# Loading the front of a two-layer graph kernel as 32-wide squares on two DMA queues

## The chip, the cores and the metric

The kernel runs on one core of a Trainium2 chip, in one launch. The metric is the device time of one execution in microseconds (us); of several executions the median counts.

## The reference

Two graph layers over N = 4096 nodes with C = 512 features. `adj` is a 4096 x 4096 matrix of zeros and ones.

```python
# layer 0: mean of the first 64 neighbours, two linear maps
keep = (adj > 0) & (cumsum(adj > 0, axis=1) <= 64);  cnt = keep.sum(axis=1)
nb_mean = (keep @ x) / max(cnt, 1)
xj = leaky_relu(nb_mean @ W_nb.T + b_nb)
xi = leaky_relu(x @ W_line.T + b_line)
x1 = layernorm(x + xi + where(cnt > 0, xj, 0))
# layer 1: graph attention
Wh = x1 @ W + bW
e  = leaky_relu((Wh @ a1 + b1)[:, None] + (Wh @ a2 + b2)[None, :], 0.2), -9e15 where adj == 0
out = layernorm(x1 + softmax(e, axis=1) @ Wh)
```

## The kernel before

The work is cut into 32 blocks of 128 rows. The order of the instructions on each engine is written out by hand; each engine goes through its own list in order, and waits only on semaphores.

**Stages.** (1) The *front* (L444 to L470) loads the first blocks of x and both weights of layer 0's maps. (2) The *maps*, L637 to L668: for each pair of blocks g, `seven(g, ...)` forms y = x W_nb^T and the line x W_line^T of two blocks with seven half-size products in place of eight (L519). (3) The *aggregation*, L726 to L766: for each block i, `keep @ y` with y split into a high and a low part (`y_hi`, `y_lo`, L758), in four groups of eight blocks; the step s counts the groups. (4) Layer 1 (L909, L1095, L1222).

**Turned operands.** TensorE contracts over partitions, so x and the weights are needed with the features on partitions. There are two ways to turn a 128 x 512 block:

- By squares: four DMAs (`load_turned_x`, L298; one for each group of 32 partitions, 64 KB, rows of 512 bytes) bring the block so that one VectorE 32 x 32 transpose (L334) ends it. The blocks 1 to 31 of x come like this.
- By TensorE: `squares` (VectorE copy, L315), four transposes by an identity matrix (`transpose_to`, L157), and a copy out of PSUM (L158, ScalarE or VectorE). x's block 0 (tile `xb`, one plain DMA of 256 KB) and the eight blocks of the two weights (`raw`, plain DMAs of 256 KB each, `load_w`, L360) come like this.

**Queues.** SP and ACT issue DMAs through hardware queues, POOL through a software queue. In the front SP issues x block 0, half of W_nb, the squares of x block 1, half of W_line, and the bias; ACT the other halves of the weights; POOL the squares of the blocks from 2 on. The hardware DMAs use eight completion semaphores in turn, over both queues together: the ninth waits until the first has landed, and so on.

**Order in the front.** TensorE first runs `spin(15)`, fifteen identity transposes, while nothing has come. Then block 0 and three blocks of W_nb are turned, and the first products run; `pys[0]`, `pys[1]` (x blocks 0 and 1 by W_nb) and `pls[0]`, `pls[1]` (by W_line) are called by `linear` (L383), each four products of 128 x 512. `pys[0]` is cut in two pieces among the transposes.

Behind them VectorE forms sums of the weights (`t1`, `t2`, `t4`, `t3`, L525, L526, L541, L542), `y_lo` (L440), turned x (L334), `line(0)` and `line(1)` (L418) and sums of x (L510 to L512). ScalarE bends the lines (L422) and copies the bias into a PSUM bank (`bank_z`, L635), which the second product of `seven(1)` adds to. Later VectorE folds W with a1 and a2 (`fold_w`, L402), and adds the line's parts (L582).

**From the maps to the aggregation.** There is no room for four of the last blocks' y while the maps run, so these are stored to `y_d` (L438) and loaded again by `room_again` (L633, 1 MB, SP's queue), which `seven(NT, True)` calls after `load_late` (three broadcast rows of 256 KB, POOL's queue). SP next issues the transposing loads of the adjacency codes, `load_kt` (L682, tile `ktb`). In the aggregation ScalarE makes `kt` from `ktb` (`make_kt`, L282), two steps ahead; in step 2 it also rounds the reloaded y to its high part (L735), after which VectorE takes the low part (L736):

```python
            make_kt(s + 2)
            if g == 2:
                bend0(i - 1)
            codes_late()
            if s == 2:
                for n in range(0, 4, 2):
                    hi, lo = (t[:, n : n + 2, :] for t in y_again)
                    nc.scalar.copy(hi, lo.bitcast(F32))
```

Of the kernel before, what the change touches and what calls it, by code (L numbers as in the profile page):

```python
# [9 lines left out]
F32 = mybir.dt.float32  # L10
F32R = mybir.dt.float32r
BF16 = mybir.dt.bfloat16
# [8 lines left out]
P = 128  # L21
SQ = 32
# [10 lines left out]
def two_layer_adj_gnn(  # L33
# [104 lines left out]
    with ExitStack() as l0:  # L138
# [8 lines left out]
        ident = big.tile([P, P], F32, name="ident")  # L147
        make_identity(nc, ident)

        def transpose_to(dst, src_of, n, wide, move):  # L150

            if wide:
                pt = ps_acc.tile([P, n, P], F32, name="acc")
            else:
                pt = ps_s.tile([P, n, P], F32, name="pt")
            for k in range(n):
                nc.tensor.transpose(pt[:, k, :], src_of(k), ident)  # L157
            move(dst, pt)  # L158

        loaded = {}  # L160
        edge_of = {}
        seen_of = {}
# [125 lines left out]
        with ExitStack() as la:  # L288
# [6 lines left out]
            xrs, xbs, xts, pys, pls = {}, {}, {}, {}, {}  # L295
            lines, held = {}, []

            def load_turned_x(i, queue=nc.gpsimd):  # L298

                if i < NB:  # L300
                    xrs[i] = late[i % 3].rearrange("p (j c) -> p j c", c=P)
                    for n in range(NC):
                        queue.dma_start(  # L303
                            xrs[i][ts(n, SQ)],
                            x_blk(i)[:, ts(n, P)].rearrange("(j a) c -> a j c", a=SQ),
                        )

            def load_own_x(i, queue):
                xbs[i] = work.tile([P, C], F32, name="xb", bufs=1) if i == 0 else late[2]
                queue.dma_start(xbs[i], x_blk(i))  # L310

            def squares(src):

                t = work.tile([P, C], F32, name="t", bufs=4)
                nc.vector.tensor_copy(  # L315
                    t.rearrange("p (m n b) -> p m n b", m=NC, b=SQ),
                    src.rearrange("p (n m b) -> p m n b", m=NC, b=SQ),
                )
                return t

            def turn_by_pe(dst, src, t=None, wide=False, move=nc.scalar.copy):
                t = squares(src) if t is None else t
                transpose_to(dst, lambda m: t[:, ts(m, P)], NC, wide, move)

            def xt_tile():
                return work.tile([P, NC, P], F32, name="xt", bufs=3)
# [1 line left out]
            def turn_x(i, t=None):  # L328
                if i < NB:
                    xts[i] = xt_tile() if t is None else t  # L330
                    if i == 0:
                        turn_by_pe(xts[i], xbs[i])
                    else:
                        nc.vector.transpose(  # L334
                            xts[i].rearrange("p m (j a) -> p j m a", a=SQ),
                            xrs.pop(i).rearrange("p j (m b) -> p j m b", b=SQ),
                        )


            def early(name):  # L340
                dt = I32 if name == "a" else BF16
                t = adj_p.tile([P, CH], dt, name=name).bitcast(F32)
                return t.rearrange("p (c q) -> p c q", q=C)

            raw = {}
            for name in ("nb", "line"):
                t = early("a")
                raw[name] = [t[:, c, :] for c in range(NC)]
            raw["w"] = []
            for k in range(2):  # L350
                t = early("left")
# [3 lines left out]
            t = early("edge")  # L355
            early_rows += [t[:, c, :] for c in range(NC // 2)]

            def load_w(name, src, queues):
                for c in range(NC):
                    queues[c % len(queues)].dma_start(raw[name][c], src[ts(c, P), :])  # L360

            def spin(n):

                idle = ps_acc.tile([P, P], F32, name="acc")
                for _ in range(n):
                    nc.tensor.transpose(idle, ident, ident)

            def turn_w(name, parts=range(NC)):

                if name not in w_t:  # L370
                    w_t[name] = wp.tile([P, NC, C], F32, name=f"wt_{name}")
                moved = [squares(raw[name][c]) for c in parts]
                for c, t in zip(parts, moved):
                    turn_by_pe(
                        w_t[name][:, :, ts(c, P)], None, t, name == "nb",
                        nc.vector.tensor_copy if name == "nb" and c == 1 else nc.scalar.copy,
                    )

            def linear(lhs_t, name, bank=None, part=slice(0, C), behind_first=lambda: None):

                pl = ps_acc.tile([P, C], F32, name="acc") if bank is None else bank
                for k in range(NC):
                    nc.tensor.matmul(  # L383
                        pl[:, part], lhs_t[:, k, :], w_t[name][:, k, part],
                        start=(k == 0 and part.start == 0),
                        stop=(k == NC - 1 and part.stop == C),
                        skip_group_check=part.stop - part.start < C,
                    )
                    if k == 0:
                        behind_first()  # L390
                return pl

            def load_rows(queue):
# [47 lines left out]
                    y_lo[i], src, y_hi[i].bitcast(F32), ALU.subtract  # L441
                )

            load_own_x(0, nc.sync)  # L444
            load_w("nb", w_nb, (nc.scalar, nc.sync))
            load_turned_x(1, nc.sync)
            load_w("line", w_line, (nc.scalar, nc.sync))
            nc.sync.dma_start(bias_line, b_line.partition_broadcast(P))
            spin(15)


            turn_x(0)
            turn_w("nb", range(3))

            for i in (2, 3):
                nc.vector.memset(late[i % 3][:, 0:1], 0.0)
                load_turned_x(i)
            pys[0] = linear(
                xts[0], "nb", part=slice(0, 3 * P), behind_first=lambda: turn_w("nb", range(3, 4))
            )  # L460
            turn_w("line", range(0, 2))
            linear(xts[0], "nb", pys[0], slice(3 * P, C))
            turn_w("line", range(2, 4))
            turn_x(1)
            load_turned_x(4)
            nc.vector.memset(raw["w"][0][:, 0:1], 0.0)
            load_w("w", w, (nc.sync,))
            load_rows(nc.sync)
            pys[1] = linear(xts[1], "nb")
            pls[0] = linear(xts.pop(0), "line")  # L470

            wide = [pls[0]]

# [154 lines left out]
            def room_again():  # L628
                for y, name in ((y_hi, "hi"), (y_lo, "lo")):
                    t = last.tile([P, ROOM, C], F32R, name=name)  # L630
                    y_again.append(t[:, 0:4, :])
                    y.update((EDGE + n, t[:, n, :]) for n in range(ROOM))
                nc.sync.dma_start(y_again[1].bitcast(F32), y_d)  # L633

            nc.scalar.copy(bank_z, bias_line)  # L635
            idle = [lambda: None] * 4
# [55 lines left out]
        def bend0(i):  # L692
            if i >= 0:
                nc.scalar.activation(fin[i], fin[i], AF.Prelu, alpha=SLOPE)
# [30 lines left out]
        make_kt(1)  # L725
        for s in range(NB * NS):  # L726
            i, g = divmod(s, NS)
            make_kt(s + 2)
            if g == 2:
                bend0(i - 1)  # L730
            codes_late()
            if s == 2:
                for n in range(0, 4, 2):
                    hi, lo = (t[:, n : n + 2, :] for t in y_again)
                    nc.scalar.copy(hi, lo.bitcast(F32))  # L735
                    nc.vector.tensor_tensor(lo, lo.bitcast(F32), hi.bitcast(F32), ALU.subtract)  # L736
            if g == 0:
                load_kt(i + 2)
                if i < 2:
                    accs[i] = ps_s.tile([P, NC, P], F32, name="pt").rearrange(  # L740
                        "p k c -> p (k c)"
                    )
                else:
                    accs[i] = ps_acc.tile([P, C], F32, name="acc")
            if g == 2:
                if i < NB - 1:
                    owns[i] = place("own")
                    nc.sync.dma_start(owns[i], x_blk(i))
            if g == 3 and i < NB - 1:
                nc.gpsimd.dma_start(owns[i], own_d[i], accum_op=ALU.add)  # L750
            kt = kts.pop(s)
            turns = list(range(KB))
            if s == NS - 1:
                turns = turns[:2] + turns[6:] + turns[2:6]
            for n, k in enumerate(turns):
                j = g * KB + k
                for term in (y_hi, y_lo):
                    nc.tensor.matmul(  # L758
                        accs[i], kt[:, k // 2, k % 2, :], term[j],
                        start=(g == n == 0 and term is y_hi),  # L760
                        stop=(g == NS - 1 and n == KB - 1 and term is y_lo),
                    )
            if g == 0:
                finish(i - 2, 4)
            finish(i - 1, g)
            codes_step(start + int((s + 1) * RATE / NS))  # L766
# [584 lines left out]
```

## Time and profile before

| | |
|---|---|
| median of 3 runs | 1555.14 us (1552.86 to 1555.37) |
| the profiled execution | 1554.29 us, of which the span of its instructions is 1552.5 us |
| TensorE (PE) | busy 1541.1 us, 99% of the span |
| VectorE (DVE), ScalarE (ACT), GpSimd (POOL) | 1266.3, 987.2 and 268.1 us |
| granted TensorE clock | 0.999 |

Times in the views count from the start of the span. The chain of waits follows the work that ended last back to what released each step. A line of the timeline gives the start, the busy time, engine, line, operation, tiles and count; `[0.75 <-DVE t L582]` is idle time ahead of it and what ended it. A matmul in 32-bit floats leaves two records. Busy times of one engine overlap a little; the distance between two starts is what an instruction takes of the engine.

### The profile page before, as it was taken

Reading aid. Unit: us, or ns where it says so; the run is one execution under the profiler, and the core shown is the slowest. Engines: PE = TensorE matmul, PEld = TensorE weight load, DVE = VectorE, ACT = ScalarE, POOL = GpSimd, SP = SyncE. Lnnn points to the kernel's source line nnn. Section 1 sums busy time; section 2 is a strip of 40 time slices with the busy share of each in tenths; the row PEclk is TensorE's granted clock in tenths of the full one; section 3 lists DMA queues with packets and bytes.
Section 4 is the critical chain, followed back from the end, with each engine's and each line's share of the span. In section 5 each row is a group of like instructions: output and inputs, shape, how many; then the busy total and the mean of one; then the engine's idle time right before and its main releaser. Section 6 shows DMA issues by size and latency. Waiting matters only on the chain.

```text
span 1552.5 us, 19129 instructions
## 1 busy us (share of the span) xinstructions
PE 1541.1 (99%) x6567; PEld 1239.6 (80%) x6567; DVE 1266.3 (82%) x2350; ACT 987.2 (64%) x1194; POOL 268.1 (17%) x428
## 2 busy tenths in 40 slices
PE   9999999999999999999999999999999999999998
PEld 5444468888888888878888888888888888888886
DVE  6988759989999899478888788888888888888864
ACT  3766668878888887427684567555675556755520
POOL 4544312222212222110001101111011110111101
PEclk9999999999999999999999999999999999999999
DMA  8965588979888886644122112222122221222201
GB/s 237 227 218 184 190 249 243 257 240 264 243 252 231 270 244 198 154 124 115 41 62 57 46 37 69 62 61 48 36 69 63 60 49 34 69 67 57 53 3 55
DMA packets 175889, 203.27 MB, mean 131 GB/s; under 512 B 102112, under 2 KB 135648, under 8 KB 167472
## 3 DMA queue, kind: packets, MB, share of 16 engines
q1 hardware_dynamic: 147616, 131.38, 29.5%
q0 software_dynamic: 26544, 68.69, 17.2%
q10 hardware_dynamic: 1632, 1.98, 0.4%
q8 instruction: 51, 0.84, 0.2%
q14 instruction: 46, 0.38, 0.1%
HBM read 142.08 MB, written 43.13 MB: 119 GB/s over the span
## 4 chain that ended last, share of the span: by engine, by line
PE 96%; DMA 2%; DVE 1%; SPq 0%; issue 0%; ACT 0%; ACTq 0%; POOLq 0%; DVEq 0%; POOL 0%
PE acc L1095 35%; PE acc L758 28%; PE pt L1095 14%; PE acc L519 12%; PE acc L909 4%; PE pt L758 1%; PE acc L383 1%; DMA ktb<-code_d 1%; DMA w<-x_d 1%; DMA a<-in_L_gnn_W_line_dram 0%; SPq L815 0%; DVE c L841 0%; DVE a L841 0%; PE pt L157 0%; DVE st L118 0%
## 5 line engine op out<-in xcount | busy, mean ns | idle before, releaser
L1095 PE MATMUL acc<-bt,s 128*128 128x256 f32 x1504 | 335.7, 379 | 0.0
L1095 PEld LDWEIGHTS acc<-bt,s 128*128 128x128 f32 x1504 | 285.8, 190 | 38.9
L758 PE MATMUL acc<-y_hi,kt 128*128 128x512 f32 x780 | 303.4, 389 | 0.0
L758 PE MATMUL acc<-y_lo,kt 128*128 128x512 f32 x780 | 303.4, 389 | 0.0
L980 ACT ACTIVATE w<-nat,few 128x1024 f32<-128x1024 uint8 x128 | 137.0, 1137 | 237.7 <-DVE a L1055 237.7
L1095 PE MATMUL acc<-bt,a 128*128 128x256 f32 x1056 | 239.0, 379 | 0.0
L1095 PE MATMUL pt<-bt,a 128*128 128x256 f32 x992 | 224.5, 379 | 0.0
L1095 PEld LDWEIGHTS acc<-bt,a 128*128 128x128 f32 x1056 | 200.6, 190 | 27.3
L1095 PEld LDWEIGHTS pt<-bt,a 128*128 128x128 f32 x992 | 188.5, 190 | 25.6
L282 ACT ACTIVATE kt<-ktb,few 128x1024 fp32r<-128x1024 uint8 x124 | 142.9, 1152 | 97.9 <-PE acc L758 78.5
L1055 DVE STREAM_TRANSPOSE a<-w 128x1024 f32<-128x1024 f32 x128 | 153.1, 1226 | 61.8 <-ACT w L1036 51.0
L127 POOL TENSOR_TENSOR rs<-ve,few 128x1 f32<-128x1 f32 x64 | 45.1, 705 | 811.1 <-DVE ve L125 798.3
L758 PEld LDWEIGHTS acc<-y_lo,kt 128*128 128x128 f32 x780 | 146.4, 188 | 30.4
L758 PEld LDWEIGHTS acc<-y_hi,kt 128*128 128x128 f32 x780 | 146.4, 188 | 30.3
L973 ACT ACTIVATE w<-w,st_n 128x1024 f32<-128x1024 f32 x128 | 149.3, 1233 | 16.1 <-DVE m L990 16.1
L1036 ACT ACTIVATE w<-w,nm 128x1024 f32<-128x1024 f32 x128 | 145.5, 1137 | 11.1 <-DVE nm L1027 11.1
L990 DVE CUSTOM_DVE_ANT_0 w<-e_n,w 128x1024 f32<-128x1024 f32 x128 | 149.5, 1221 | 1.3
L179 ACT ACTIVATE edge<-a,few 128x2048 bf16<-128x2048 int32 x64 | 136.3, 2129 | 0.5 <-DMA a<-in_adj_dram 0.5
L227 ACT CAST code<-left 128x2048 uint8<-128x2048 bf16 x64 | 121.1, 1893 | 0.0
L210 DVE TENSOR_TENSOR left<-edge,left 128x2048 bf16<-128x2048 bf16 x64 | 78.4, 1225 | 2.2
L198 DVE TENSOR_TENSOR_SCAN left<-few,ends,left 128x1024 bf16<-128x1024 f32 x32 | 75.2, 2351 | 1.1
L303 POOL DMA_DIRECT2D c<-in_x_dram x120 | 65.8, 555 | 57.0 <-DVE xt L334 40.7
(236 smaller groups left out, 2059.2 us busy)
## 6 DMA issues: line engine op xcount, KB each, us to landing
a<-in_adj_dram SPq DMA_DIRECT2D x64, 1024.0 KB, 6.0
code_d<-code POOLq DMA_DIRECT2D x64, 256.0 KB, 4.0
nat<-code_d SPq DMA_DIRECT2D x248, 64.0 KB, 2.2
w<-x_d SPq DMA_DIRECT2D x128, 64.0 KB, 2.1
own<-in_x_dram SPq DMA_DIRECT2D x31, 256.0 KB, 3.3
own<-own_d POOLq DMA_DIRECT2D x31, 256.0 KB, 5.2
x_d<-own POOLq DMA_DIRECT2D x31, 256.0 KB, 4.8
c<-in_x_dram POOLq DMA_DIRECT2D x120, 64.0 KB, 5.0
```

Of the source, the lines that this page charges most:

```text
L179: nc.scalar.activation(edge_of[s], loaded.pop(s).rearrange("p (t q) -> p q t", q=2), AF.Sigmoid, bias=steep[:, 0:1], scale=STEEP, accum_ou ...
L210: nc.vector.tensor_tensor(left, e, left, ALU.mult)
L227: nc.scalar.copy(code.bitcast(U8).rearrange("p (t q) -> p q t", q=2), seen_of.pop(s))
L282: nc.scalar.activation(kts[s], bytes_.rearrange("p t (i r) -> p t r i", r=2), AF.Sigmoid, bias=steep[:, 1:2], scale=STEEP,)
L519: nc.tensor.matmul(bank, lhs[:, k, :], rhs[:, k, :], start=start and k == 0, stop=k == 1, skip_group_check=True,)
L758: nc.tensor.matmul(accs[i], kt[:, k // 2, k % 2, :], term[j], start=(g == n == 0 and term is y_hi), stop=(g == NS - 1 and n == KB - 1 and ...
L973: nc.scalar.activation(dst, src, AF.Prelu, bias=bias, scale=scale, alpha=0.2)
L980: nc.scalar.activation(wts[b][:, i, :], nats[b, i // 2].bitcast(U8)[:, i % 2, :], AF.Relu, bias=far, scale=-FAR,)
L990: nc.vector.tensor_tensor_reduce(w_i, e2_n, w_i, 1.0, -3e38, ALU.subtract, ALU.max, m4s[b][:, i : i + 1])
L1036: nc.scalar.activation(w_i, w_i, AF.Exp, bias=nms[b][:, i : i + 1], accum_out=z4s[g][:, r, i : i + 1])
L1055: nc.vector.transpose(a[:, r].rearrange("p s (i a) -> p i s a", a=SQ), wts[2 * g + r][:, :, ts(k, 8 * SQ)].rearrange("p i (s x) -> p i s x ...
L1095: nc.tensor.matmul(banks[g][n], lhs[:, j, :], bt[:, 4 * k + j, rhs, :], start=(k == 0 and j == 0 and n == mate[0]), stop=(k == NP - 1 and ...
```

## The change

Block 0 of x and both weights now come as squares too. `load_squares` is the general form of the four DMAs; its list `queues` gives the first two groups of partitions (0 to 63) to SP and the other two (64 to 127) to ACT. A weight comes in two halves of 256 rows, each four DMAs of 128 KB. The order of issue on both queues is x block 0, W_nb's halves, x block 1, W_line's halves, x block 2, then x block 3, which waits until block 0 is turned. On each queue that is two DMAs of each item. POOL's queue loads x from block 4 on.

Weights are turned by VectorE in quarters (128 rows, `turn_quarter`), and `by_quarters` has one quarter of the product (four of 128 x 128) follow each: for `pys[0]` and for `pls[0]`. Fifty-four instructions go: nine VectorE copies, 36 TensorE transposes and nine copies out of PSUM (eight of them on ScalarE). `spin` has 24 transposes. The bias, W and the rows follow on SP's queue behind the squares.

At the other end, the reload of y goes from SP's queue to POOL's, behind `load_late`, and the rounding of y in step 2 stands ahead of `make_kt(4)`.

```diff
-            def load_turned_x(i, queue=nc.gpsimd):
+            def load_squares(dst, src, queues):
+                for n in range(NC):
+                    queues[n * len(queues) // NC].dma_start(
+                        dst[ts(n, SQ)], src[:, ts(n, P)].rearrange("(j a) c -> a j c", a=SQ)
+                    )
+
+            def turn_squares(dst, src):
+                nc.vector.transpose(
+                    dst.rearrange("p m (j a) -> p j m a", a=SQ),
+                    src.rearrange("p j (m b) -> p j m b", b=SQ),
+                )
+
+            def load_turned_x(i, queues=(nc.gpsimd,)):
...
-            def load_w(name, src, queues):
-                for c in range(NC):
-                    queues[c % len(queues)].dma_start(raw[name][c], src[ts(c, P), :])
+            def load_half(name, src, h):
+                load_squares(raw[name][:, ts(h, 2 * NC)], src[ts(h, 2 * P), :], both)
...
-            def turn_w(name, parts=range(NC)):
...
+            def turn_quarter(name, c):
+                turn_squares(w_t[name][:, :, ts(c, P)], raw[name][:, ts(c, NC)])
+
+            def by_quarters(lhs_t, name):
+                bank = None
+                for c in range(NC):
+                    turn_quarter(name, c)
+                    bank = linear(lhs_t, name, bank, slice(P * c, P * c + P))
+                return bank
...
-            load_own_x(0, nc.sync)
-            load_w("nb", w_nb, (nc.scalar, nc.sync))
-            load_turned_x(1, nc.sync)
-            load_w("line", w_line, (nc.scalar, nc.sync))
-            nc.sync.dma_start(bias_line, b_line.partition_broadcast(P))
-            spin(15)
-
-
-            turn_x(0)
-            turn_w("nb", range(3))
-
-            for i in (2, 3):
-                nc.vector.memset(late[i % 3][:, 0:1], 0.0)
-                load_turned_x(i)
-            pys[0] = linear(
-                xts[0], "nb", part=slice(0, 3 * P), behind_first=lambda: turn_w("nb", range(3, 4))
-            )
-            turn_w("line", range(0, 2))
-            linear(xts[0], "nb", pys[0], slice(3 * P, C))
-            turn_w("line", range(2, 4))
+            both = (nc.sync, nc.scalar)
+            load_turned_x(0, both)
+            for h in range(2):
+                load_half("nb", w_nb, h)
+            load_turned_x(1, both)
+            for h in range(2):
+                load_half("line", w_line, h)
+            load_turned_x(2, both)
+            spin(24)
+
+            turn_x(0)
+            load_turned_x(3, both)
+            nc.sync.dma_start(bias_line, b_line.partition_broadcast(P))
+            pys[0] = by_quarters(xts[0], "nb")
             turn_x(1)
             load_turned_x(4)
+            pys[1] = linear(xts[1], "nb")
             nc.vector.memset(raw["w"][0][:, 0:1], 0.0)
-            load_w("w", w, (nc.sync,))
+            for c in range(NC):
+                nc.sync.dma_start(raw["w"][c], w[ts(c, P), :])
             load_rows(nc.sync)
-            pys[1] = linear(xts[1], "nb")
-            pls[0] = linear(xts.pop(0), "line")
+            pls[0] = by_quarters(xts.pop(0), "line")
...
-                nc.sync.dma_start(y_again[1].bitcast(F32), y_d)
+                nc.gpsimd.dma_start(y_again[1].bitcast(F32), y_d)
...
-            make_kt(s + 2)
-            if g == 2:
-                bend0(i - 1)
-            codes_late()
             if s == 2:
                 for n in range(0, 4, 2):
                     hi, lo = (t[:, n : n + 2, :] for t in y_again)
                     nc.scalar.copy(hi, lo.bitcast(F32))
                     nc.vector.tensor_tensor(lo, lo.bitcast(F32), hi.bitcast(F32), ALU.subtract)
+            make_kt(s + 2)
+            if g == 2:
+                bend0(i - 1)
+            codes_late()
```

More of the change, by code (lines that the diff above doesn't have):

```diff
@@ L148, in two_layer_adj_gnn @@
         make_identity(nc, ident)
[L150 to L158, printed above, removed]
         loaded = {}
@@ L296, in two_layer_adj_gnn @@
             lines, held = {}, []
-            def load_turned_x(i, queue=nc.gpsimd):
+            def load_squares(dst, src, queues):
[9 more added lines that the diff above has]
+            def load_turned_x(i, queues=(nc.gpsimd,)):
                 if i < NB:
                     xrs[i] = late[i % 3].rearrange("p (j c) -> p j c", c=P)
[L302 to L305, printed above, removed]
-                        )
+                    load_squares(xrs[i], x_blk(i), queues)
             def load_own_x(i, queue):
-                xbs[i] = work.tile([P, C], F32, name="xb", bufs=1) if i == 0 else late[2]
+                xbs[i] = late[2]
                 queue.dma_start(xbs[i], x_blk(i))
[L312 to L323, printed above, removed]
             def xt_tile():
@@ L330, in turn_x @@
                     xts[i] = xt_tile() if t is None else t
[L331 to L337, printed above, removed]
+                    turn_squares(xts[i], xrs.pop(i))
             def early(name):
-                dt = I32 if name == "a" else BF16
-                t = adj_p.tile([P, CH], dt, name=name).bitcast(F32)
+                t = adj_p.tile([P, CH], BF16, name=name).bitcast(F32)
                 return t.rearrange("p (c q) -> p c q", q=C)
@@ L346, in two_layer_adj_gnn @@
             for name in ("nb", "line"):
-                t = early("a")
-                raw[name] = [t[:, c, :] for c in range(NC)]
+                t = adj_p.tile([P, CH], I32, name="a").bitcast(F32)
+                raw[name] = t.rearrange("p (j q) -> p j q", q=P)
+                w_t[name] = wp.tile([P, NC, C], F32, name=f"wt_{name}")
             raw["w"] = []
@@ L366, in spin, with linear @@
                     nc.tensor.transpose(idle, ident, ident)
-            def turn_w(name, parts=range(NC)):
[L370 to L379, printed above, removed]
+            def turn_quarter(name, c):
[6 more added lines that the diff above has]
+                return bank
+            def linear(lhs_t, name, bank=None, part=slice(0, C)):
                 pl = ps_acc.tile([P, C], F32, name="acc") if bank is None else bank
@@ L388, in linear @@
                     )
-                    if k == 0:
-                        behind_first()
                 return pl
@@ L442, in y_terms @@
                 )
-            load_own_x(0, nc.sync)
-            load_w("nb", w_nb, (nc.scalar, nc.sync))
-            load_turned_x(1, nc.sync)
-            load_w("line", w_line, (nc.scalar, nc.sync))
-            nc.sync.dma_start(bias_line, b_line.partition_broadcast(P))
-            spin(15)
-            turn_x(0)
-            turn_w("nb", range(3))
-            for i in (2, 3):
-                nc.vector.memset(late[i % 3][:, 0:1], 0.0)
-                load_turned_x(i)
-            pys[0] = linear(
-                xts[0], "nb", part=slice(0, 3 * P), behind_first=lambda: turn_w("nb", range(3, 4))
-            )
-            turn_w("line", range(0, 2))
-            linear(xts[0], "nb", pys[0], slice(3 * P, C))
-            turn_w("line", range(2, 4))
+            both = (nc.sync, nc.scalar)
[9 more added lines that the diff above has]
+            load_turned_x(3, both)
+            nc.sync.dma_start(bias_line, b_line.partition_broadcast(P))
+            pys[0] = by_quarters(xts[0], "nb")
             turn_x(1)
             load_turned_x(4)
+            pys[1] = linear(xts[1], "nb")
             nc.vector.memset(raw["w"][0][:, 0:1], 0.0)
-            load_w("w", w, (nc.sync,))
+            for c in range(NC):
+                nc.sync.dma_start(raw["w"][c], w[ts(c, P), :])
             load_rows(nc.sync)
-            pys[1] = linear(xts[1], "nb")
-            pls[0] = linear(xts.pop(0), "line")
+            pls[0] = by_quarters(xts.pop(0), "line")
             wide = [pls[0]]
```

## The prediction

> **What bounds the kernel now.** First the page, for the engine that sets the end; then busy time by stage.
>
> ```profile
> span 1552.5 us, 19129 instructions
> PE 1541.1 (99%) x6567; PEld 1239.6 (80%) x6567; DVE 1266.3 (82%) x2350; ACT 987.2 (64%) x1194; POOL 268.1 (17%) x428
> ```
>
> ```profile
> 0.00:14.20 14.20, 11.98 (x67) 10.19 (x68) 5.30 (x20) 4.91 (x8) 6.37 (x16) 1.00 0.88 247
> 26.60:206.00 179.40, 179.37 (x418) 79.22 (x419) 151.02 (x247) 116.88 (x150) 81.41 (x150) 1.00 0.66 198
> 206.00:221.00 15.00, 14.24 (x62) 11.15 (x61) 3.91 (x5) 8.58 (x10) 2.14 (x4) 1.00 1.06 298
> ```
>
> Columns: stretch, length, then PE, PEld, DVE, ACT, POOL busy, clock, DMA share, GB/s. PE has no idle time in the maps. So whatever brings the maps forward brings the end forward, unless another engine cannot follow. In the first 14.2 us PE is busy too, but partly with work that is no product: spinning and transposes. The chain of waits shows what the front hangs on:
>
> ```profile
> 1.67 5.90 DMA a<-in_L_gnn_W_line_dram
> 8.46 0.91 PE acc L383 x2
> 11.75 0.87 PE pt L157 x8
> 14.39 10.32 PE acc L383 x24
> 24.73 0.70 DVE t L418
> 26.62 15.48 PE acc L519 x35
> ```
>
> Products are in pieces among transposes until 14.2 us; then `pys[1]`, `pls[0]`, `pls[1]` run unbroken to 24.7. From there line(1), its bend and the bank's copy lead into the maps. The aggregation's start, by the same view:
>
> ```profile
> 206.98 9.18 DMA ktb<-code_d
> 217.32 1.04 ACT hi L735
> 218.38 1.24 DVE lo L736
> ```
>
> **The front on TensorE.** The timeline of PE gives every price:
>
> ```profile
> 1.37 3.46 PE L366 MATMUL acc<-ident 128*128 128x128 f32 x15 [1.37 <-POOL ident masks.py:199]
> 12.46 1.06 PE L383 MATMUL acc<-wt_nb,xt 128*128 128x128 f32 x8
> 13.35 1.04 PE L157 MATMUL pt<-ident,t 128*128 128x128 f32 x8
> 14.22 3.60 PE L383 MATMUL acc<-wt_nb,xt 128*128 128x512 f32 x8
> 17.66 7.03 PE L383 MATMUL acc<-wt_line,xt 128*128 128x512 f32 x16
> ```
>
> A spin transpose costs 3.46/15 = 0.231 us; 24 from 1.37 end at 6.91. A quarter (four 128 x 128 products, eight records) costs 13.35 − 12.46 = 0.89, a whole map 17.66 − 14.22 = 3.44. If data never lack: 6.91 + 4 x 0.89 = 10.47 for `pys[0]`, + 3.44 = 13.91 for `pys[1]`, + 3.56 = 17.47 for `pls[0]`, + 3.44 = 20.91 for `pls[1]`. Before, the same point is 17.66 + 2 x 3.44 = 24.54. The bound of the gain is 3.63 us. Cutting `pls[0]` into quarters costs 0.12 of it, counted here.
>
> **Whether data lack.** Up to W_line's second half 0.26 + 1.05 + 0.26 + 1.05 = 2.62 MB come. x block 4 (0.26 MB, POOL's queue) may run beside them, since block 1 is turned by about 10 us: 2.88 MB. The rows of 512 bytes decide the rate. Two stretches of the DMA view, the first with rows of 2 KB alone, the second mostly with squares (367 − 55 = 312 of 416 packets):
>
> ```profile
> DMA packets 662, 1.22 MB, mean 371 GB/s; under 512 B 64, under 2 KB 64, under 8 KB 662
> DMA packets 416, 0.26 MB, mean 260 GB/s; under 512 B 55, under 2 KB 367, under 8 KB 416
> ```
>
> In the densest half microsecond of squares (7.7 to 8.2 us) it is 234 GB/s. Data start at about 2.2 us (the first issue is at 0.75; the stretch's slices fill from there), and a landing is seen about 0.5 later. I take 260, the nearest row: 2.2 + 2.88/0.26 = 13.3, seen at 13.8. Ends: 371 GB/s gives 10.5, 234 gives 15.0. W_nb is through at 2.2 + 1.31/0.26 + 0.5 = 7.7; its third quarter is turned at 8.4, when PE (second quarter done at 8.69) has only just come to it. x block 1 is seen at 8.7, its turn comes behind the fourth quarter, at 9.7. So `pys[1]` does not wait.
>
> VectorE then decides. Behind W_line's second half it has, by distances of starts: two quarters and x block 2, 3 x 0.63; `t1`, `t2` 2.41; two `y_lo` 1.30; x block 3 0.64; line(0) 0.57; three sums 1.20: 8.0 us. line(1) can start at 13.8 + 8.0 = 21.8; PE would allow 21.1. Before it starts at 24.73: 2.9 us earlier (3.6 at 371 GB/s, 1.7 at 234). VectorE is dense from there, and PE meets it again soon:
>
> ```profile
> 40.54 0.30 PEld L519 LDWEIGHTS acc<-hi,xt 128*128 128x128 f32 x2 [0.75 <-DVE t L582]
> ```
>
> so VectorE's 2.9 and not PE's 3.6 goes into the end. Behind that PE has no stall to 206.
>
> What else moves in the front: ACT issues 16 DMAs at about 0.45 us, but its first copy is `y_hi`, which waits for `pys[0]` anyway; 8 copies out of PSUM, 0.59 each, leave it. The bias now stands behind all squares on SP. By the semaphores it issues at about 15 and, at the 4.3 us to landing that the DMA view shows for it, is there at 19.3; line(0) wants it at about 20. W, a1 and the adjacency issue some 3 us later than before; `fold_w` wants its rows at 25, and edge(0) wants the adjacency at 34 to 35, where it lands by about 31. These cost nothing; with the cover gone (bias at 21) line(0) would give back 1 us.
>
> A rule speaks against this front. The Trainium skill, page "DMA: Bandwidth & Descriptors", section "Bandwidth", calls transfers under 64 KB dominated by their descriptors and gives 138 GB/s at 64 KB; by that, an estimate, 2.88 MB would take 20.9 us, line(1) would start near 31.6, and the kernel would lose 7. The row of 260 GB/s, where 64 KB squares were most of the packets, decides. For the division of the queues, the row is that one queue's squares alone ran at 234 GB/s. The page "SBUF — State Buffer", section "Door 1: The DMA port swizzle", says that partitions 0 to 63 reach only half of the 16 ports and 64 to 127 the other half; by that, SP's and ACT's squares together should exceed 234.
>
> **The reload of y.** In the timeline of PE
>
> ```profile
> 218.46 0.44 PE L758 MATMUL pt<-hi,kt 128*128 128x512 f32 x1
> 219.66 0.50 PE L758 MATMUL pt<-lo,kt 128*128 128x512 f32 x1 [0.76 <-DVE lo L736]
> ```
>
> neighbours elsewhere are 0.227 apart. From 218.46 to 221.36 are seven steps, 1.59, in 2.90 us: 1.31 lost. ACT's rounding stands behind `make_kt(4)`, which waits for `ktb` until 216.26, while y has landed at 205.69 + 6.9 = 212.6. In the new order the rounding waits only for y. But y now issues at about 207.3, behind 0.79 MB of rows on POOL's queue and beside two transposing loads (1.05 MB): 2.9 MB in all, which the stretch moved at 298 GB/s, so 206.9 + 9.7 = 216.6 if y is last, 206.9 + 1.84/0.298 = 213.1 if its queue goes first. Middle: about 215; then the low part is ready at 217.3, the product wants it at 217.78, and nearly all of the 1.31 goes. At 216.6 some 0.7 is saved. I take 0.9. `make_kt(4)` ends at about 218.5, wanted at 221. The transposing loads on SP no longer stand behind 1 MB, which has no price: kt(4) has 2 us to spare.
>
> **Sum.** 2.9 + 0.9 = 3.8 against the profiled execution's 1554.29: 1550.5 (its span less 3.8, and the same 1.8 around it). It lies 0.85 below the median of the runs, so 1551.3 is the forecast. A measurement of this kernel tells some 0.2%, 3.1 us, from no change; that is 1552.0 to 1558.3.
>
> **Rivals.** *Data come as fast as PE takes them* (300 GB/s and more, both halves of the ports in use): 3.6 + 1.3 = 4.9, 1550.2. For it: each queue serves other partitions. Against: W_line's squares meet x block 4. 30%.
>
> *The front lands slowly, and the gain shrinks below 3.1*: 234 GB/s gives 1.7, and y as late as 216.6 gives 0.7: 2.4, 1552.7. The kernel would count as the same. 25%.
>
> *Four semaphores to a queue starve the front* (slower). Each queue may have four squares in flight; the fifth waits for the first to land. SP shows such waits now:
>
> ```profile
> SPq L303 <- DMA a<-in_L_gnn_W_nb_dram: 2.6, 2, 2.1
> ```
>
> So x block 0, W_nb's second half, W_line's first half and x block 2 follow one another, landing by landing. At the 4.3 us that the squares on SP take to land now, block 2 is there at 0.75 + 17.2 = 17.95, and line(1), 6.7 behind it, at 24.7: no gain in the front, 1554.2. At the 6.2 us of W_line's loads on ACT it is 25.6 and 32.3: 7.6 late, less 0.9, so 1561.8. The kernel counts as slower from 5.3 us a landing on (22.0, line(1) 4.0 late). Against it: such landings are long where bytes wait for bytes, and then the rate is full; squares with little beside them land in 2.1 (the page's 128 loads of `w`). Four landings of 3.5 fit the forecast's 14.8. 11%.
>
> The change does what it says: the waits of the new order show no wait of VectorE or PE other than for the squares.
>
> **Chances.** The forecast 34%, the fast rival 30%, the small gain 25%, the starved front 11%. The forecast's own lower edge (1551.3 + 0.7) touches 1552.0, so I leave 2 of its points to no change: faster 0.62, same 0.27, slower 0.11. The range takes the fast rival's 1550.2 less 0.5 for a median's luck, and the small gain up to no front gain at all (1555.14 − 0.7 = 1554.4): 1549.7 to 1554.5.
>
> **What would show it.** In the new profile: `pls[1]` ends near 21; line(1) starts at 21 to 22 and waits for PE or follows VectorE's sums without a gap; the last W_line squares land near 13.8; no idle PE between 6.9 and 20.9; near 215 the reload, and PE without the 0.76. Wrong would be: VectorE waiting for W_line beyond 17 us, PE waiting longer at L582 than before, or ACT's rounding waiting for y beyond 217.

## The result: slower, and the profile after

The changed kernel takes 1569.42 us (median of 7 runs, 1560.91 to 1574.83), the kernel before beside it 1554.2; the ratio is 1.009 (95% interval 1.0062 to 1.0118). The forecast was 1551.3, faster. The profiled execution, 1560.91 us, is the fastest of the seven, so it shows only a part of the loss.

In this execution the front did what the prediction says. From the timelines of PE and VectorE, changed kernel:

```profile
14.70 7.17 PE L360 MATMUL acc<-wt_line,xt 128*128 128x128 f32 x40
```

```profile
14.09 1.31 DVE L295 STREAM_TRANSPOSE wt_line<-a 128x512 f32<-128x512 f32 x2 [0.97 <-DMA a<-in_L_gnn_W_line_dram]
21.96 0.68 DVE L393 TENSOR_TENSOR t<-acc,bias_line 128x512 f32<-128x512 f32 x1
26.52 0.69 DVE L377 SCALAR_TENSOR_TENSOR edge<-left,code 128x512 f32<-128x512 f32 x1 [0.98 <-DMA code<-in_L_gnn_a_dram]
28.02 0.69 DVE L377 SCALAR_TENSOR_TENSOR edge<-left,code 128x512 f32<-128x512 f32 x1 [0.81 <-DMA code<-in_L_gnn_a_dram]
```

W_line's second half is turned from 14.09 (forecast 13.8), `pls[1]` ends at 21.7, and line(1), the second line, starts at 21.96, 2.77 earlier than before. That is the earliest of the twelve profiled executions with the new front (this one and those of the runs below): the others turn that half from 14.18 to 15.23 and start line(1) from 22.57 to 23.93 (the four with the old front: 24.04 to 25.27). Then 1.79 is given back: `fold_w` waits for a1 and a2, which now come behind W and the squares. PE meets VectorE again at L552 (L582 before), as busy stretch and wait show:

```profile
39.64 1.98 PE L489 MATMUL acc<-hi,xt 128*128 128x512 f32 x4 [0.80 <-DVE t L552]
```

That product started at 40.54 before. The 0.90 stays, as PE's timeline shows for the aggregation's first product, before and after:

```profile
205.62 0.50 PE L758 MATMUL pt<-y_hi,edge 128*128 128x512 f32 x1
```

```profile
204.72 0.50 PE L728 MATMUL pt<-y_hi,edge 128*128 128x512 f32 x1
```

One pair of executions does not show a gain of that size: the four profiled old fronts (this one, e3, e4 and e10 below) scatter from 204.93 to 206.15 at this point.

Then the reload, first as the DMA view of before has it (KB, us from issue to landing), then in the changed kernel: busy time by stretch (columns as before: length, PE, PEld, DVE, ACT, POOL, clock, DMA share, GB/s), the chain of waits, and PE's timeline:

```profile
lo<-y_d SPq DMA_DIRECT2D x1, 1024.0 KB, 6.9
```

```profile
206.00:221.00 15.00, 11.72 (x52) 9.37 (x50) 0.65 (x2) 2.95 (x3) 0.87 (x2) 1.00 1.11 136
221.00:240.00 19.00, 14.99 (x58) 11.99 (x59) 15.06 (x21) 15.93 (x15) 1.49 (x3) 0.82 1.16 267
224.50:228.50 4.00, 3.49 (x8) 2.46 (x9) 3.94 (x4) 4.00 (x4) 0.89 (x1) 0.52 1.07 313
```

```profile
206.34 17.09 DMA lo<-y_d
225.81 17.56 PE pt L728 x71
```

```profile
217.34 0.39 PE L728 MATMUL pt<-lo,kt 128*128 128x512 f32 x1
224.55 0.79 PE L728 MATMUL pt<-hi,kt 128*128 128x512 f32 x1 [6.82 <-ACT hi L701]
225.81 0.79 PE L728 MATMUL pt<-lo,kt 128*128 128x512 f32 x1 [0.47 <-DVE lo L702]
226.82 0.63 PE L728 MATMUL pt<-lo,kt 128*128 128x512 f32 x1
227.25 0.63 PE L728 MATMUL pt<-hi,kt 128*128 128x512 f32 x1
```

The reload takes 17.09 us; 6.9 before. In its stretch the DMA moves 136 GB/s where it moved 298, with its engines no less busy (1.11 against 1.06). PE waits 6.82 + 0.47, and then its products are 0.43 apart instead of 0.227, until 228.5; the granted clock from 224.5 to 228.5 is 0.52. The 128 products end at 225.81 + 17.56 = 243.37, 38.65 after the first. Unbroken they take 29.31 (the rounding alone, e4 below): 9.34 lost, of which 7.29 are the waits and 2.05 the halved clock. Before, 30.66, so 1.35 lost. Sum: −0.90 + 9.34 − 1.35 = +7.1; the spans differ by 6.6, so half a microsecond comes back later.

The Trainium skill, page "TensorE: Matmul & The Clock Gate", section "Part 1: The HAM clock gate", says that the clock falls to half after an idle window of about 3.4 us and comes back after as long a busy one. The 6.82 idle and the steps of 0.43 agree. The length of the idle time does not bear it out as a threshold: in e12 and e13 below the granted clock falls to 0.5 for 3.4 us after idle times of 2.05 and 1.91. The measurement decides.

### The profile page after: what moved, and what is told of

It reads as the page before. It is cut to its first block, busy times and chain, and to the rows that moved or that the text cites. A ratio compares the mean times of both kernels' runs of the same rounds, so it can differ in the third digit from the quotient of the medians.

```text
span 1559.1 us, 19160 instructions
## 1 busy us (share of the span) xinstructions
PE 1540.4 (99%) x6580; PEld 1240.9 (80%) x6580; DVE 1267.3 (81%) x2347; ACT 982.6 (63%) x1186; POOL 264.6 (17%) x421
## 4 chain that ended last, share of the span: by engine, by line
PE 93%; DMA 3%; DVE 1%; issue 1%; ACT 0%; POOL 0%; ACTq 0%; SPq 0%; POOLq 0%; DVEq 0%
PE acc L1065 35%; PE acc L728 28%; PE pt L1065 14%; PE acc L489 10%; PE acc L879 5%; PE pt L728 1%; DMA lo<-y_d 1%; DMA c<-in_x_dram 1%; DMA code<-in_L_gnn_a_dram 1%; DMA nat<-code_d 0%; DMA a<-in_L_gnn_W_nb_dram 0%; DMA a<-in_L_gnn_W_line_dram 0%; ACT code L217 0%; DMA e_d<-w 0%; POOL own_d L404 0%
## 5 line engine op out<-in xcount | busy, mean ns | idle before, releaser
L1065 PE MATMUL pt<-bt,a 128*128 128x256 f32 x992 | 224.5, 379 | 0.0
L188 DVE TENSOR_TENSOR_SCAN left<-few,left 128x1024 bf16<-128x1024 f32 x32 | 73.3, 2292 | 1.1
```

Of the source, the lines that this page charges most:

```text
L188: nc.vector.tensor_tensor_scan(left[:, 1], three.to_broadcast([P, CH // 2]), left[:, 0], NEIGHBORS + 3.0 if h == 0 else end, ALU.max, ALU. ...
L1065: nc.tensor.matmul(banks[g][n], lhs[:, j, :], bt[:, 4 * k + j, rhs, :], start=(k == 0 and j == 0 and n == mate[0]), stop=(k == NP - 1 and ...
```

## The experiments

"Spread" is lowest to highest. The medians of before in the four groups were 1553.9, 1554.3, 1554.2 and 1553.5.

| run | front | reload on | rounding | store of `wa` | median us (spread) | ratio, 95% interval |
|---|---|---|---|---|---|---|
| e4 | old | SP | new order | 35 us | 1552.8 (1552.0–1555.7) | 0.9995 [0.9986, 1.0003] |
| e10 | old | SP | new order | late | 1553.3 (1552.2–1555.8) | 0.9996 [0.9987, 1.0005] |
| e3 | old | POOL | new order | 35 us | 1565.1 (1562.0–1567.7) | 1.0076 [1.0063, 1.0089] |
| e2 | new | SP | old order | 35 us | 1558.1 (1552.7–1563.0) | 1.0023 [1.0008, 1.0037] |
| e1 | new | SP | new order | 35 us | 1553.1 (1551.5–1561.3) | 1.0002 [0.9990, 1.0014] |
| e7 | new, rows first | SP | new order | 35 us | 1558.7 (1553.2–1563.1) | 1.0025 [1.0013, 1.0038] |
| e5 | new | ACT | new order | 35 us | 1557.4 (1552.0–1563.9) | 1.0020 [1.0004, 1.0035] |
| e8 | new | SP | new order | late | 1551.1 (1549.8–1552.4) | 0.9977 [0.9968, 0.9986] |
| e9 | new, rows first | SP | new order | late | 1552.2 (1551.3–1554.6) | 0.9984 [0.9975, 0.9993] |
| e11 | new | POOL | new order | late | 1563.6 (1561.5–1567.3) | 1.0064 [1.0050, 1.0078] |
| e12 | new | POOL, transposes held | new order | late | 1556.3 (1554.3–1557.5) | 1.0013 [1.0004, 1.0021] |
| e15 | new | POOL, ahead of rows | new order | late | 1552.9 (1551.1–1554.7) | 0.9995 [0.9985, 1.0004] |
| e13 | new | ACT | new order | late | 1551.6 (1550.4–1554.8) | 0.9983 [0.9974, 0.9992] |
| e14 | new | ACT, further behind | new order | late | 1551.7 (1550.8–1553.9) | 0.9989 [0.9979, 0.9998] |

**The change taken apart.** e1 is the changed kernel with the reload back on SP; e2 has the new front alone; e3 the old front with the reload and the rounding changed; e4 the rounding alone.

```diff
-                nc.gpsimd.dma_start(y_again[1].bitcast(F32), y_d)
+                nc.sync.dma_start(y_again[1].bitcast(F32), y_d)
```

> The changed kernel with the reload of y back on SP's queue; front and order of the rounding stay as changed. Theory A (the reload on POOL's queue, beside the transposing loads, is what costs; the front gains 0.9 us): PE's 6.8 us wait for the rounding (ACT hi) is gone, the reload lands about 7 us after its issue, the rounding starts near 212, the 1.31 us of stall that the kernel before has there goes too; 1552 us, about 2 below before. Theory B (the rounding ahead of make_kt(4) is what costs, since ScalarE then waits for y with kt behind it): PE still waits several us there, 1558 or more. Theory C (the front upsets the load traffic all the way to the maps' end): the reload stays slow, over 12 us, 1558 or more.

> The front of the change alone: the reload on SP and the rounding behind make_kt(4), as before. A: maps end 0.9 us sooner than before (204.7 in place of 205.6), the stall of 1.31 us at the reloaded blocks stays; 1553.4, 0.9 below before. B: the same. C: slower than before by some us.

> The kernel before with the other two edits alone: reload on POOL's queue, rounding ahead of make_kt(4). A: the reload lands 15 us or more after its issue, PE waits 7 us and more for ACT hi, time 1562 to 1575 and spread as the changed kernel is. B: the same. C: no such wait, about 1553.

> The kernel before with the rounding ahead of make_kt(4) alone; the reload stays on SP. A: the rounding starts at 212.6, when y has landed, the low part is ready before PE wants it, 1.31 us of stall go: 1553, 1.0 to 1.3 below before. B: PE loses several us, 1558 or more.

The reload's queue carries the loss: e3 has it with the old front, and PE waits 6.4 there for ACT's rounding. The rounding ahead of `make_kt(4)` is harmless, as e4's chain shows:

```profile
205.23 29.31 PE pt L758 x128
```

PE is unbroken, so the 1.35 that were lost there are gone; the median is 1.1 lower, though the interval alone does not exclude no change. e2 is slower than before by some microseconds, the number of theory C and not its place: the reload lands in time. What none of the theories foresaw is the spread of the new front: 5 of e2's 12 runs lie within 1552.7 to 1553.9, the others between 1557.5 and 1563. e2's profiled execution, 1562.96, shows where, in VectorE's timeline and in the DMA view of 38 to 48 us:

```profile
45.26 0.71 DVE L295 STREAM_TRANSPOSE lo<-c 128x512 f32<-128x512 f32 x1 [7.51 <-DMA c<-in_x_dram]
```

```profile
DMA packets 136, 0.24 MB, mean 24 GB/s; under 512 B 98, under 2 KB 98, under 8 KB 115
```

VectorE waits 7.51 for a square of x, PE behind it 7.95, and again PE's clock is halved behind that (in the mean 0.63 from 39 to 49 us, 0.87 from 49 to 60). The DMA stands nearly still. It does so in the kernel before as well, in the same stretch:

```profile
DMA packets 123, 0.18 MB, mean 18 GB/s; under 512 B 81, under 2 KB 81, under 8 KB 120
```

Ahead of it lies one transfer, `fold_end`'s store `wa_d<-wa` on SP (36.47 us before, 35.04 in e2): 1,024 elements of 4 bytes, each a packet of its own. By the semaphores that it waits for, VectorE's turn at 45.26 needs the four squares that POOL issued between 26.63 and 29.08. Each lands in 16 parts; of the last square 15 parts were in by 36.24, and the sixteenth came at 45.18. In the kernel before, the same four (issued from 28.60 to 30.25) were in by 34.55, ahead of the store. The stretch from 32 to 36 us, before and in e2, shows what holds them up:

```profile
32.00:36.00 4.00, 4.00 (x11) 1.78 (x10) 3.86 (x11) 0.59 (x1) 1.27 (x3) 1.00 0.29 83
```

```profile
32.00:36.00 4.00, 4.00 (x11) 1.80 (x10) 3.90 (x11) 0.30 (x1) 1.02 (x2) 1.00 0.85 254
```

Before, the loads are nearly through and the DMA moves 83 GB/s; in e2, with W, the rows and the adjacency issued later, it still moves 254. So either the store halts the queues, or the shifted loads alone do.

**The store moved, the rows first.** e7 puts the rows ahead of W; e8 stores `wa` in the eighth pair of blocks (86 us; it is read at 205); e9 does both.

```diff
-                nc.sync.dma_start(wa_d.rearrange("k (c p) -> p k c", p=P), wa)
...
+                if g == 8:
+                    store_wa()
                 seven(g, False, steps)
```

```diff
+            load_rows(nc.sync)
             for c in range(NC):
                 nc.sync.dma_start(raw["w"][c], w[ts(c, P), :])
-            load_rows(nc.sync)
```

> The changed front with the reload on SP's queue, but the rows a1, a2 and b_w (and b1, b2) issued ahead of W's four loads. Theory R (the order of the loads decides fold_w): in the changed kernel fold_w waited 0.98 and 0.81 us for a1 and a2; here both waits go to under 0.2 us, PE's first product on the other half of x starts some 1.8 us earlier, and a good run is at 1550 to 1551 us. Theory S (the store of wa, 1,024 elements of 4 bytes, halts every queue for some 10 us, and x's squares must land ahead of it): here the store is issued even earlier, so more of the squares come too late, VectorE waits 5 us and more at its turn of x near 40 us, and the median is no better than 1553, with runs above 1557. Rival T (the poor runs of the front come from something else than this store): waits of fold_w go and no run is above 1555.

> The changed front with the reload on SP's queue, and the store of wa taken from near 35 us to the eighth pair of blocks (some 110 us), where the kernel only needs it by 205 us. Theory S (the store halts the queues and the front's late loads run into it): the stretch from 36 to 48 us shows the DMA moving over 200 GB/s, x's squares land in under 5 us, VectorE waits less than 1 us near 40 us, and all runs lie within 3 us of each other, at 1550.5 to 1552.5 us; a stretch of 10 us with the DMA nearly still appears near 110 us instead, and costs little there. Rival T (the poor runs come of the shifted loads of the adjacency and W alone): two groups of runs remain, near 1552 and near 1560, as in the front alone.

> Both: rows ahead of W and the store of wa in the eighth pair, with the changed front and the reload on SP's queue. Theories R and S together: 1549 to 1551 us, all runs within 3 us, which would beat the kernel before by 3 to 5 us. If S is wrong, two groups remain; if R is wrong, no gain on the kernel with the late store alone.

With the store away, the spread is 2.6 us instead of 9.8, and the median 1551.1, 2 us under e1 and better than both kernels. The DMA view of e8, first 38 to 48 us, then 92 to 100:

```profile
DMA packets 681, 2.84 MB, mean 284 GB/s; under 512 B 197, under 2 KB 197, under 8 KB 473
DMA packets 106, 0.36 MB, mean 45 GB/s; under 512 B 20, under 2 KB 20, under 8 KB 105
```

The standstill has moved along with the store, to a place where nothing waits for it. And its chain is whole:

```profile
205.40 29.33 PE pt L732 x128
```

The rows first are another matter. In e7 the wait for a1 and a2 goes, but `fold_w` waits 1.10 for W in its place, and VectorE then stands 6.10 before x's square at 44.85; in e9, where the store is late, fold_w waits only 0.16, and the time does not improve on e8. VectorE's timeline of e9:

```profile
39.11 0.71 DVE L295 STREAM_TRANSPOSE lo<-c 128x512 f32<-128x512 f32 x1 [1.28 <-DMA c<-in_x_dram]
```

So behind the rows the next late thing is x's square on POOL's queue, and theory R's gain does not come. It was a weak test: in e8, without the rows first, `fold_w` waits only 0.56 (0.32 and 0.24), not 1.79.

e10 is the control, the old front with rounding and late store:

> The kernel before, with the rounding of y ahead of make_kt in the fourth step and the store of wa in the eighth pair; its front is the old one. Theory F (the new front is worth some 1.5 us as soon as nothing holds up its late loads, and the move of the store by itself gives the old front nothing, as its squares of x landed ahead of the store): 1552.3 to 1553.3 us, as the rounding alone (1552.8), against 1551.1 of the new front with both. Rival G (the gain of the new front with the late store came of the store): 1550.8 to 1551.5 us.

1553.3 against e4's 1552.8: the move of the store brings the old front nothing, and by these medians the new front without the collision is worth 1553.3 − 1551.1 = 2.2 us. That is the upper end: over e8, e9, e13 and e14 against e4 and e10 it is between 0.6 and 2.2. The profiled executions do not show it. The aggregation starts at 205.23 in e4, 206.15 in e10 and 205.40 in e8; over the nine new fronts that the store's standstill does not catch it starts from 203.81 to 206.32, and in the middle at 205.4, as over the four old ones.

**The reload: queue, or neighbours?** e5 (store early) and e13 (late) have it on ACT's queue; e11 is the changed kernel with the late store; e12 holds SP's transposes back with a store of 64 KB from the reloaded tile:

```diff
+        nc.sync.dma_start(hold_d, y_again[1][:, 0, 0:P].bitcast(F32))
         load_kt(1)
```

> The changed kernel with the reload of y on ACT's queue instead of POOL's. Theory A1 (any two queues suffer when the transposing loads run beside plain ones): the reload takes 15 us or more from issue to landing, PE waits over 5 us for the rounding, 1560 to 1570 us. Theory A2 (only the software queue of POOL is starved by the transposes): the reload lands within 9 us, by 216, PE waits under 1 us, 1552 to 1555 us.

> The changed kernel as it is, reload of y on POOL's queue, but with the store of wa in the eighth pair: what the reload's new queue costs with the front's spread gone. Theory A (the reload on POOL's queue shares the DMA with SP's transposes): it takes 14 to 18 us to land, PE waits 4 to 8 us for the rounding, then runs at half its clock for some us, and the time is 1560 to 1565 us, 9 to 13 above the 1551.1 with the reload on SP. Rival (most of the loss of the change was in the front): under 1556 us.

> As the last, but SP first issues a small store of 64 KB from the reloaded tile, which has to wait for the reload, so that the transposes start behind it: POOL's queue has the DMA to itself. Theory A (it is the transposes beside it that make the reload slow): the reload lands in 6 to 9 us, PE's wait for the rounding is gone or under 1 us; the two transposes come some 7 us later, which puts kt(4) near 222 to 226 us and may cost PE up to 5 us there; 1551 to 1557 us. Rival B (POOL's software queue is slow by itself with 1 MB): the reload takes 14 us and more as before, and the time is over 1562 us.

> The changed kernel with the store of wa in the eighth pair and the reload on ACT's queue, issued behind ACT's two rounds of y, some 1 us later than on ACT alone and so behind the issue of SP's first transpose. Theory A3 (whichever comes second waits: a plain load issued behind transposes is held up, on every queue): the reload takes over 12 us, PE waits 3 us and more, 1557 to 1565 us. Theory A2 (only POOL's software queue is held up): it takes under 10 us, 1551 to 1553 us.

e5 has the front's spread in it; its reload landed in 7.0 us and PE did not wait there. e11 against e8 is the clean price of the queue: 12.4 us. PE's wait and the reload in e11 (by the views of waits and of the chain), and the reload in e12, by the DMA view:

```profile
PE pt L732 <- ACT hi L705: 8.6, 1, 8.6
205.43 18.88 DMA lo<-y_d
```

```profile
lo<-y_d POOLq DMA_DIRECT2D x1, 1024.0 KB, 9.3
```

Without transposes beside it the reload on POOL takes 9.3, of which 4.1 pass behind the three broadcasts before its first packet (210.61); the wait for the rounding is gone. e12 still loses, because the transposes now come late: PE waits 2.0 for kt, and its clock is halved behind that (0.58 from 222.9 to 226.8). So POOL's queue is not slow by itself. But on ACT (6.7 in e13) the reload also came ahead of the transposes: issued at 206.49, they at 207.66. e13's expectation took it for the other order, so it does not tell its theories apart. The last two runs were to separate queue from order:

```diff
             make_kt(s + 2)
+            if s == 1:
+                nc.scalar.dma_start(y_again[1].bitcast(F32), y_d)
```

```diff
-            seven(NT, True, [idle[0], idle[0], lambda: make_kt(0), load_late])
+            seven(NT, True, [idle[0], idle[0], lambda: make_kt(0), idle[0]])
+            load_late()
```

> The changed kernel with the store of wa in the eighth pair and the reload on ACT's queue, but issued behind ACT's third sigmoid of make_kt, some 3 us behind the issue of the transposes, so that their packets are under way first. Theory Q (it is POOL's queue that suffers beside transposes; ACT's does not): the reload lands in 5 to 9 us from its issue, by 218, PE waits under 2 us, 1551 to 1554 us. Theory O (what comes behind the start of the transposes is held up, on any queue): 12 us or more from issue to landing, PE waits over 5 us, 1560 us and more.

> The changed kernel with the store of wa in the eighth pair and the reload on POOL's queue, ahead of the three broadcasts of load_late (b_nb and wa's two rows, 256 KB each) instead of behind them, 1.6 us earlier and ahead of the transposes' first packet. Theory O (what starts first goes through): the reload lands within 9 us, PE waits under 1 us, 1551 to 1553 us. Theory Q (POOL's queue suffers beside transposes, in either order): it takes 13 us and more, PE waits over 2 us, 1556 us and more.

e15 settles it for POOL: on the same queue, but ahead of the broadcasts and so of the transposes (issued at 204.97 against 206.03; in e11 at 205.43 against 205.16), the reload lands in

```profile
lo<-y_d POOLq DMA_DIRECT2D x1, 1024.0 KB, 6.4
```

By the packet records its first packet starts at 206.62 and the transposes' first at 210.33, when it is nearly done; in e11 theirs started at 209.35 and its own at 209.74. 10.7 us of e11's time are gone. The broadcasts do not explain that: in e12 the reload stood behind them too. e14 missed its aim. Its reload stands behind three sigmoids in ACT's list, but the timeline of ACT has it issued ahead of them:

```profile
205.84 0.59 ACT L416 CAST hi<-acc 128x512 fp32r<-128x512 f32 x1
205.99 0.36 ACTq L708 DMA_DIRECT2D lo<-y_d  x1
206.80 3.24 ACT L272 ACTIVATE kt<-a,few 128x1024 fp32r<-128x1024 uint8 x3
```

Whether a plain load on a hardware queue, begun behind transposes, suffers as POOL's does stays open.

## Why the prediction was wrong

- **The reload, the step that failed.** The prediction let 2.9 MB pass at the 298 GB/s of before, in whatever order, and had y there at 213.1 to 216.6. It landed at 223.43. The sentence at fault is "The transposing loads on SP no longer stand behind 1 MB, which has no price". Standing behind that megabyte was what kept the transposes from running beside it. The 298 GB/s were a row in which SP's queue did reload and transposes one after the other; beside each other, in the reload's last stretch (212 to 222), they moved 119. Cost by e11 and e8: 12.4 us. The Trainium skill, page "DMA: Bandwidth & Descriptors", section "Issuing engines are not separate DMA queues", has the DMAs of all engines interleave on the same 16 DMA engines; the overlap here agrees, and the section gives no price for it. Its section "Rules for kernel authors" says that a transpose next to ordinary DMAs needs nothing; that row is about correct data, and for the time e11 and e8 show that it needs room.
- **"These cost nothing."** W, a1 and the adjacency 3 us later were priced at zero because each was thought to have slack to its own reader. The rows had none: in the changed kernel `fold_w` waits 1.79 for a1 and a2. And what was not asked is whom they meet: POOL's squares of x, late beside them, are caught by the `wa` store's standstill. Cost by medians: changed kernel 1569.4 less e11's 1563.6 = 5.9 us, with a wide spread.
- **The front: its mechanism was right, its size too large.** 14.09 for 13.8 and 21.96 for 21.8 were the luck of the execution that was profiled: in the middle of the twelve, line(1) starts at 23.0, which the prediction's sum gives for its slow bound (15.0 and 8.0 behind it). The rate was mis-sized: from 2.2 to 13.6 us the DMA moves 244 GB/s in the changed kernel and 226 in e8, where the forecast has 260. That is above the estimate of 138 and not clearly above the 234 of one queue's squares. The term of 2.9 came out as 0.6 to 2.2 by medians. PE's idle time before 20.9 was 0.64, not none.
- **The rounding was right**: 1.1 by medians (e4), 0.9 forecast, with the reload where it had been.
- **The rivals.** The slower one put its loss on four semaphores in the front; the squares and weights landed in 3.7 us in the middle, 4.8 at most, near the forecast's 3.5 and under the 5.3 that it needs. Its side was right and its mechanism not. The test named for being wrong, ACT's rounding waiting for y beyond 217, is what the profile shows: 223.45.

With the two collisions avoided, e8 is at 1551.1, beside the forecast's 1551.3. That is partly luck: it lies 3.2 under its own before, not 3.8, and e9, e13 and e14, with no such collision either, are at 1551.6 to 1552.2.

## What to carry to other kernels

A transfer that starts ahead of others also keeps them away from its neighbours. When it moves to another queue, ask what will now run beside it, and do not price the mix at the rate of the sequence. When loads shift, look at what they meet on the way, not only at the slack to their readers. A wide spread of runs points at such a race: find the transfer that some runs pass ahead of and others behind.

## What the hardware showed

- A store of 1,024 elements of 4 bytes, 4 KB in all, leaves the DMA nearly still for 8 to 10 us, on both queues that had work, POOL's and SP's (18 GB/s before, 24 in e2; 45 over 8 us in e8's later place). By the packet records of before, the small packets themselves start between 37.40 and 38.08 and take 7 ns each; the stall follows: the next 16 packets of 4 KB on POOL's queue take 3.4 to 9.5 us, 6.6 in the mean. Why is not shown, nor whether it is the size of the elements.
- Plain packets of 8 KB beside transposing ones of 256 bytes (e11, 210 to 216 us): most take what they take alone, 316 ns for 309 and 18 ns for 18, but some take up to 6.6 and 1.4 us, so the means are 1,260 and 70 ns. Between 210 and 216 us, 63 plain packets are under way; in e12, without transposes, 128 take from 210.6 to 215.2.
- ACT issues a DMA while older operations of its list have yet to end: in e14 two casts, one of them running, and three sigmoids. Five older operations did not delay it there; a longer list was not tried.
- 7 us of idle time cost TensorE another 2 at half its clock (changed kernel); idle times of 2.05 (e12) and 1.91 us (e13) already halve it for 3.4.
